# Graph layer with segment max: the dsts' clamp, the masks and the sum of x rearranged in the kernel's front

## The chip, the cores and the metric

The kernel runs on one core of a Trainium2 chip. Its engines work side by side, each through its own list of instructions in order: TensorE (PE in the profile, with its weight loads as PEld), VectorE (DVE), ScalarE (ACT), GpSimd (POOL) and SyncE (SP), which here only starts transfers. An engine waits where an instruction needs a semaphore that another engine or a transfer sets. The metric is the device time of one execution in microseconds. The kernel before took 811.47 us as the median of 3 runs (811.27 to 813.49).

## The reference

The input x has 6250 nodes of 128 channels. There are 206,250 edges as two lists, src and dst, sorted by dst (both directions of 100,000 random edges, and one self edge for each node). With W of 128 x 256 and b of 128:

```python
h = jnp.maximum(_layernorm(x, axis=-1), 0.0)
x_i, x_j = h[dst], h[src]
feat = jnp.concatenate([x_i, x_j - x_i], axis=-1)
msg = feat @ W.T + b
out = jax.ops.segment_max(msg, dst, num_segments=x.shape[0])
return x + jnp.where(jnp.isfinite(out), out, 0.0)
```

Split W into its halves W1 and W2. Then a message is A[dst] + B[src] + b with A = h (W1 - W2)^T and B = h W2^T. A[dst] + b is the same for all edges of a node, so the result is x + A + b + the maximum of B over the node's sources. The kernel computes A and B for all nodes once; the rest is a maximum over gathered rows.

## The kernel before, in words

**Tiling.** Node rows lie in a tile `xs` (the first 125 partitions of HX) as 125 partitions of Q = 50 nodes each, loaded in five groups of ten columns (`GQ`). For the edges, each of the 128 partitions owns LD = 49 consecutive nodes and reads a window of WIN = 1792 consecutive edges, which holds all its edges. Edges whose src is no duplicate within a look-back of POS = 44 go into one-hot matrices, which the main loop turns into B columns by matmuls; duplicates, at most 512 in a window, go into lists and are handled by gathers of B rows.

**Order.** The schedule is manual: each engine's instructions stand in the order of the text. The front (up to 177 us) does, with names and lines of the profile:

- *Constants* on POOL and VectorE: identities `ident`, `identb`, the negated `nid` and `nidb` (scaled by 1024), iotas, and `crow` and `rows_` (L317 to L321), one-partition rows for the selection table `Sel`.
- *Windows.* The last dst of each of 375 blocks is read (L330 to L341), a block is gathered, the count of smaller dsts gives the window's beginning (L386 to L391), and two gathers fetch `swin` (srcs) and `dwin` (dsts). `after` (L266) writes one element of the next x columns from the data that has just come, so that the x load behind it waits for that data: the second group of ten columns behind the block, groups three to five behind `dwin`.
- *Moments.* `moments` (L352) computes mean and variance of ten columns on VectorE, `roots` the square root on ScalarE, `scales` the reciprocal. Groups one and two run before the first comparison, three to five between comparisons.
- *Layernorm steps.* `ln_to(n)` issues steps up to number n. Step k works on five pairs of columns at once, as a pipeline: `ln_rest` of pair k-4, `ln_mul` of k-3, `ln_low` of k-2, `ln_turn` of k-1, `ln_scale` of k. `ln_mul` multiplies a split into a high and a low part by a split W, ten matmuls of 256 columns (L477), adds x through an identity matmul (L478), and ScalarE copies the results to `Bp`, the store buffer `b2` and, as A + b + x, back into `xs`. After each fifth pair SP stores ten columns of B to Bt and of `xs` to XA. 29 steps in all.
- *Keys and comparisons.* ScalarE forms `dlf` = dst - 49 p + 1 in place (L516); VectorE clamps it to 0..50 as `dlc` (L519), splits src into quotient and rest (`q16`) and packs dst and rest into a 16-bit key `KA`, with a copy `KB` shifted by one place. For each of 44 distances VectorE compares the keys with themselves (L552) into one of three buffers, and `count` adds the result into `dup` in PSUM by four matmuls (L541). Two masks are counted with weight -1024 so that marked places never pass as duplicates: `out_` (edges of other partitions' nodes) and `selfm` (self edges, L561), both after the 44 comparisons.
- *Lists.* `res` = (dup > 0) (L571), a running count, and eleven shift steps (L592, L593) pack the duplicates to the left; a one-column matmul with `tri` gives each partition's offset, which VectorE reads at the ninth step (L596). The lists are scattered to memory (`Lt`, L607, from POOL) and read back as balanced rows (L612, L629), from which the 432 gathers of the main loop take their indices. `turned` transposes q16, dlc and the values into TQ, TD, TV for the one-hots (`build`, L148).
- *Checks.* `same`, `junk` and others (L650 to L697) count violations of what the kernel assumes of the data; a sum above zero starts a slow general path.

**The main loop** (325 pairs) makes one-hots, multiplies them with Bp, takes maxima in `acc` on VectorE and streams 432 gathered duplicate rows. XA is read at the end and added.

Of the kernel before, what the change touches and what calls it, by code (L numbers as in the profile page):

```python
# [8 lines left out]
F32 = mybir.dt.float32  # L9
F32R = mybir.dt.float32r  # L10
BF16 = mybir.dt.bfloat16
# [4 lines left out]
ALU = mybir.AluOpType  # L16
# [34 lines left out]
def gnn_kernel(tc, x, src, dst, W, b, out):  # L51
# [28 lines left out]
    with ExitStack() as ctx:  # L80
# [20 lines left out]
        with ExitStack() as body:  # L101
# [137 lines left out]
            with ExitStack() as pre:  # L239
# [64 lines left out]
                for i, v in enumerate((-0.5 * LD - 0.5, -0.25 * (LD * LD - 1), float(-L))):  # L304
                    G_.memset(shifts[:, i:i + 1], v)
# [10 lines left out]

                V.tensor_tensor(crow[:, 0], crow[:, 0], crow[:, 0], ALU.mult)  # L317
                V.tensor_scalar(crow[:, 0], crow[:, 0], -1.0, 1.0, op0=ALU.mult, op1=ALU.add)
                V.tensor_scalar(crow[:, 1], crow[:, 0], -2047.0, -2048.0, op0=ALU.is_lt, op1=ALU.mult)
                V.tensor_tensor(rows_[:, 3], crow[:, 0], crow[:, 1], ALU.subtract)  # L320
                V.tensor_copy(rows_[:, 2], crow[:, 1])  # L321
# [46 lines left out]
                brow = pool.tile([P, 2 * C], F32R, name="brow")  # L368
# [14 lines left out]
                V.tensor_tensor(brow[32:33, C:], bsrc[32:33], brow[32:33, C:].bitcast(F32), ALU.subtract)  # L383
# [3 lines left out]
                after(V, blk_f[:1], GQ)  # L387
# [10 lines left out]


# [34 lines left out]

# [5 lines left out]
                V.memset(lw[96:], 0.0)  # L440
# [29 lines left out]
                def ln_mul(k):  # L470
                    st = steps[k]
                    st["pm"] = ps_m.tile([P, 2, 2 * C], F32, name="pm")
                    for j in range(2):
                        o = st["pm"][:L, j]
                        hi, lo = (slot(i, k)[:, j, :L] for i in (1, 2))
                        for a, w in ((bsel, brow), (hi, whi), (hi, wlo), (lo, whi), (lo, wlo)):
                            T_.matmul(o, a, w, start=j == 0 and a is bsel, stop=True, skip_group_check=True)  # L477
                    T_.matmul(st["pm"][:L, :, C:], ident[:L, :L], xs[:, 2 * k:2 * k + 2], start=False, stop=True,  # L478
                              skip_group_check=True)
# [28 lines left out]
                dlf = dwin.bitcast(F32)  # L508
# [7 lines left out]
                A_.activation(dlf, dwin, AF.Identity, bias=nthr)  # L516
                V.tensor_scalar(v16, big, MAGIC, -MAGIC, op0=ALU.add, op1=ALU.add)
                V.scalar_tensor_tensor(q16, v16, float(-Q), swin, op0=ALU.mult, op1=ALU.add)
                V.tensor_scalar(dlc, dlf, 0.0, float(LD + 1), op0=ALU.max, op1=ALU.min)  # L519
# [23 lines left out]
                for s in range(1, POS + 1):  # L543
                    e = eqs[s % 3]
                    if s in (12, 24):
                        turned(*((q16, TQ) if s == 12 else (dlc, TD)))
# [6 lines left out]
                    count(identb, e, first=s == 1)  # L553
                    for g, s0 in ((2, 8), (3, 14), (4, 20)):
# [5 lines left out]
                    ln_to(6 + 9 * s // POS)  # L560
# [378 lines left out]
```

## Time and profile before

| | us |
|---|---|
| median of 3 runs | 811.47 |
| the profiled execution | 809.35 |
| its span, first to last instruction | 807.6 |
| VectorE busy | 734.2 (91%) |
| TensorE busy | 662.4 (82%) |
| ScalarE busy | 511.8 (63%) |
| GpSimd busy | 502.5 (62%) |
| start of the first comparison (L552) | 37.39 |
| start of `res` (L571) | 101.63 |
| start of the scatter of the lists (L607) | 149.09 |
| end of the checks on VectorE | 177.0 |

Times in the profile count from the first instruction. A row of a timeline gives start, duration in us, engine, line, operation, output and input, and in brackets the idle time before it on its engine with what ended that. In the chain of waits a row is start, duration and what ran; it follows one chain back from the last instruction. Matmuls overlap one another, so their durations add up to more than the time between their starts.

### The profile page before, as it was taken

How to read it: one execution, taken by the hardware profiler on the slowest of the kernel's cores; microseconds unless marked ns; L12 is line 12 of the kernel's file. 1: busy time of each engine (PE TensorE's matmuls, PEld its weight loads, DVE VectorE, ACT ScalarE, POOL GpSimd, SP SyncE). 2: the span in 40 equal slices, each digit the busy share in tenths (PEclk: the TensorE clock that was granted, in tenths of full speed). 3: DMA queues.
4: the chain of work that ended last, by engine and by line, in shares of the span. 5: the costliest groups of instructions: out<-in, count | busy, mean ns of one | idle time of the engine just before them, and what ended most of it. 6: DMA issues, size and time to landing. Idle time of an engine off the chain costs nothing.

```text
span 807.6 us, 12060 instructions
## 1 busy us (share of the span) xinstructions
PE 662.4 (82%) x3646; PEld 434.2 (54%) x3646; DVE 734.2 (91%) x1368; ACT 511.8 (63%) x1130; POOL 502.5 (62%) x538
## 2 busy tenths in 40 slices
PE   1688977259898998799989998989989999989950
PEld 0455766138765565455555555555555555556730
DVE  6698899888789899999999999999999999998972
ACT  2664487046789999667575766666576666657800
POOL 5200000377777777777777777777777777774773
PEclk9999999559999899799999999999999999999975
DMA  4631222312333333333333373333343333334152
GB/s 126 178 106 46 64 65 71 99 47 79 93 87 105 102 105 101 106 104 102 102 102 105 101 190 106 101 103 103 107 114 105 108 105 103 102 104 124 54 161 84
DMA packets 79650, 82.09 MB, mean 102 GB/s; under 512 B 11699, under 2 KB 68503, under 8 KB 79223
## 3 DMA queue, kind: packets, MB, share of 16 engines
q1 hardware_dynamic: 63038, 46.54, 20.4%
q0 software_dynamic: 15840, 33.93, 14.8%
q10 hardware_dynamic: 700, 0.78, 0.5%
q8 instruction: 30, 0.49, 0.2%
q14 instruction: 42, 0.34, 0.1%
HBM read 42.34 MB, written 38.82 MB: 100 GB/s over the span
## 4 chain that ended last, share of the span: by engine, by line
DVE 41%; PE 23%; issue 17%; ACT 10%; DMA 5%; POOL 2%; DVEq 0%; POOLq 0%; SPq 0%; ACTq 0%
DVE acc L798 16%; PE ps L787 10%; DVE rows L223 9%; ACT oh L739 4%; PE z L738 4%; PE dup L541 3%; DVE acc L593 3%; DMA rows<-Bt,lists 3%; PE pv L189 2%; DMA rows<-M,last_e 2%; ACT dump L810 2%; POOL rows L77 1%; ACT Vb L199 1%; ACT Vsq L198 1%; DVE acc L592 1%
## 5 line engine op out<-in xcount | busy, mean ns | idle before, releaser
L77 POOL DMA_INDIRECT rows<-Bt,lists x432 | 437.2, 1012 | 137.4 <-DMA rows<-Bt,lists 44.5
L739 ACT ACTIVATE oh<-z 126x490 fp32r<-126x490 f32 (+1 forms) x650 | 336.7, 574 | 156.7 <-PE z L738 149.6
L787 PE MATMUL ps<-oh,Bp 126*128 126x490 f32 (+1 forms) x1300 | 390.2, 423 | 23.4 <-DVE acc L798 16.2
L798 DVE TENSOR_TENSOR acc<-acc,ps 128x980 f32<-128x980 f32 (+1 forms) x312 | 359.2, 1151 | 23.4 <-PE ps L787 19.7
L787 PEld LDWEIGHTS ps<-oh,Bp 126*128 126x128 f32 x1300 | 235.3, 193 | 147.5 <-DVE acc L798 90.7
L738 PE MATMUL z<-Vb,Sel 128*128 128x490 f16 (+1 forms) x650 | 194.7, 378 | 14.7 <-ACT oh L739 8.8
L223 DVE SCALAR_TENSOR_TENSOR rows<-rows,lists 128x128 f32<-128x128 f32 x431 | 148.0, 343 | 1.4 <-DMA rows<-Bt,lists 0.4
L189 PEld LDWEIGHTS <-HX 128*128 128x128 bf16 x896 | 68.3, 159 | 52.7 <-issue 37.3
L189 PE MATMUL pv<-HX 128*128 128x28 bf16 (+1 forms) x826 | 74.0, 232 | 16.2 <-ACT Vb L199 16.2
L607 POOL DMA_INDIRECT Lt<-big,where_i x1 | 1.0, 1037 | 120.4 <-DVE big L606 120.4
L738 PEld LDWEIGHTS <-Sel 128*128 128x128 f16 x650 | 43.1, 104 | 55.5 <-issue 53.9
L166 DVE TENSOR_TENSOR HX<-T,IQ 128x700 bf16<-128x700 bf16 x128 | 65.5, 515 | 0.0
L77 POOL DMA_INDIRECT rows<-M,last_e x40 | 38.2, 956 | 12.2 <-issue 7.0
L541 PE MATMUL dup<-rows,identb 128*128 128x512 bf16 (+1 forms) x176 | 36.7, 352 | 4.4 <-DVE rows L552 3.9
L810 ACT ACTIVATE dump<-lists,nbias 128x512 bf16<-128x512 f32 x50 | 37.0, 741 | 0.1
L541 PEld LDWEIGHTS <-identb 128*128 128x128 bf16 x176 | 17.0, 97 | 21.2 <-issue 6.1
L552 DVE TENSOR_TENSOR rows<-KA,KB 128x1792 bf16<-128x1792 int16 x22 | 23.8, 1082 | 3.7 <-PE dup L541 3.7
L477 PE MATMUL pm<-whi,lhl 128*125 128x256 f32 x100 | 26.6, 287 | 0.0
L477 PE MATMUL pm<-wlo,lhl 128*125 128x256 f32 x100 | 26.5, 287 | 0.0
L552 DVE TENSOR_TENSOR rows<-KA 128x1792 bf16<-128x1792 int16 x21 | 22.8, 1085 | 1.4 <-PE dup L541 1.4
L454 ACT ACTIVATE rows<-HX,nmr,rstd 125x128 f32<-125x128 f32 x50 | 22.8, 525 | 1.1 <-DVE rows L440 1.1
L173 DVE TENSOR_TENSOR HX<-HX,T 128x392 bf16<-128x392 bf16 x64 | 23.2, 363 | 0.3
(239 smaller groups left out, 564.4 us busy)
## 6 DMA issues: line engine op xcount, KB each, us to landing
M<-rows SPq DMA_DIRECT2D x54, 512.0 KB
rows<-Bt,lists POOLq DMA_INDIRECT x432
HX<-in_x SPq DMA_DIRECT2D x5, 560.0 KB
Bt<-acc SPq DMA_DIRECT2D x5, 560.0 KB
XA<-HX SPq DMA_DIRECT2D x5, 560.0 KB
out_x<-rows SPq DMA_DIRECT2D x4, 448.0 KB
xa<-XA SPq DMA_DIRECT2D x1, 1512.0 KB
T<-XA SPq DMA_DIRECT2D x1, 1176.0 KB
```

The costliest lines, as they stand in the source:

```text
L77: G_.indirect_dma_start(out=o, out_offset=None, in_=table, in_offset=bass.IndirectOffsetOnAxis(ap=idx, axis=0))
L166: V.tensor_tensor(oh, over(TQ, z - a), iq, ALU.is_equal)
L189: T_.matmul(o2[:, :, lo:lo + w], OHQ[:, :, i], OHD[:, :, :, i], start=False, stop=True, skip_group_check=True)
L223: V.scalar_tensor_tensor(G[:, j], state["prev"], slim[:, k:k + 1], G[:, j], op0=ALU.min, op1=ALU.max)
L477: T_.matmul(o, a, w, start=j == 0 and a is bsel, stop=True, skip_group_check=True)
L541: T_.matmul(dup[:, c0:c1], m, e[:, c0:c1], start=first, stop=last)
L552: V.tensor_tensor(e, KA[:, 64:], i1, ALU.is_equal)
L738: T_.matmul(z[:, :n], Sel[:, Q - 1 - i - j], Vb[t % 2][:, :n], start=True, stop=True)
L739: A_.activation(oh[:, :n], z[:L + 1, :n], AF.Relu)
L787: T_.matmul(ps[:, j, :n], Bp[:, e, i + j], oh[j][:, :n], start=e == 0, stop=e == 1)
L798: V.tensor_tensor(a, a, ps[:, :, :n], ALU.max)
L810: A_.activation(dump, sdl, AF.Sign, scale=2.0, bias=nbias[:, c:c + 1], accum_out=ends[:, c:c + 1])
```

## The change

What it does, part by part:

- The second group of x's columns is loaded behind `dwin` like groups three to five, and its moments stand behind the first comparison; groups three, four and five behind comparisons 9, 17 and 25.
- The `crow` operations and the clearing of `lw` stand behind the window gathers on VectorE.
- `dlc` comes from the integer `dwin` by two VectorE operations and now reaches from 0.5 to 49.5; the key is 128 dlc + q16. ScalarE's pass in place is gone.
- ScalarE writes `sl16`, src - 49 p + 1 in 16 bits. `selfm` is a 16-bit comparison of dlc with it, at comparison 9; `out_` is counted at comparison 6. Both use the space of TV, so KB stays the key.
- XA is filled with x by two copies in memory, on SP ahead of the stores of Bt. The identity matmul goes, the bias row is twice as wide and one matmul serves both columns; `xs` becomes A + b, and POOL adds it to XA by transfers that accumulate.
- Four layernorm steps stand ahead of the first comparison and six among the comparisons, against six and nine; the rest follows behind them. The transposes of q16 and dlc follow the last step.
- The `same` operations stand behind the read-back of the lists. Two one-column operations on dlc go.

```diff
-                V.tensor_tensor(crow[:, 0], crow[:, 0], crow[:, 0], ALU.mult)
...
-                    A_.copy(brow[r:r + 1, C:], bsrc[r:r + 1])
+                    A_.copy(brow[r:r + 1], bsrc[r:r + 1].rearrange("r (o c) -> r o c", o=1).to_broadcast([1, 2, C]))
...
-                after(V, blk_f[:1], GQ)
...
+                V.tensor_tensor(crow[:, 0], crow[:, 0], crow[:, 0], ALU.mult)
...
+                V.memset(lw[96:], 0.0)
...
-                moments(GQ, 2 * GQ)
-                roots(GQ, 2 * GQ)
-                scales(GQ, 2 * GQ)
-                for q0 in range(2 * GQ, Q, GQ):
+                for q0 in range(GQ, Q, GQ):
                     after(G_, dwin, q0)
...
                 nc.sync.dma_start(M_v[:, 0], none)
+                for l0, l1 in ((0, N // P * P), (N // P * P, N)):
+                    o, i = (a[l0:l1].rearrange("(p r) c -> p (r c)", p=min(P, l1 - l0)) for a in (XA, x))
+                    nc.sync.dma_start(o, i)
...
+                    T_.matmul(st["pm"][:L, :, C:], bsel, brow, start=True, stop=True, skip_group_check=True)
                     for j in range(2):
-                        o = st["pm"][:L, j]
                         hi, lo = (slot(i, k)[:, j, :L] for i in (1, 2))
-                        for a, w in ((bsel, brow), (hi, whi), (hi, wlo), (lo, whi), (lo, wlo)):
-                            T_.matmul(o, a, w, start=j == 0 and a is bsel, stop=True, skip_group_check=True)
-                    T_.matmul(st["pm"][:L, :, C:], ident[:L, :L], xs[:, 2 * k:2 * k + 2], start=False, stop=True,
-                              skip_group_check=True)
+                        for a, w in ((hi, whi), (hi, wlo), (lo, whi), (lo, wlo)):
+                            T_.matmul(st["pm"][:L, j], a, w, start=False, stop=True, skip_group_check=True)
...
                             nc.sync.dma_start(Bt_l[p0:p1, q0:q0 + GQ], bo[p0:p1])
-                            nc.sync.dma_start(XA_l[p0:p1, q0:q0 + GQ], xs[p0:p1, q0:q0 + GQ])
+                            G_.dma_start(XA_l[p0:p1, q0:q0 + GQ], xs[p0:p1, q0:q0 + GQ], accum_op=ALU.add)
...
-                selfm = KB[:, :WIN].bitcast(BF16)
...
-                out_ = TV.rearrange("p s b -> p (s b)")
-                ln_to(4)
+                out_ = selfm = TV.rearrange("p s b -> p (s b)")
...
-                A_.activation(dlf, dwin, AF.Identity, bias=nthr)
...
-                V.tensor_scalar(dlc, dlf, 0.0, float(LD + 1), op0=ALU.max, op1=ALU.min)
-                V.scalar_tensor_tensor(KA[:, 64:], dlc, 64.0, q16, op0=ALU.mult, op1=ALU.add)
+                V.tensor_scalar(dlc, dwin, nthr, 0.5, op0=ALU.add, op1=ALU.max)
+                V.tensor_scalar_min(dlc, dlc, LD + 0.5)
+                V.scalar_tensor_tensor(KA[:, 64:], dlc, 128.0, q16, op0=ALU.mult, op1=ALU.add)
                 V.tensor_copy(KB[:, 64:], KA[:, 63:63 + WIN])
-                ln_to(6)
+                ln_to(4)
...
+                sl16 = sh_.bitcast(BF16)[:, :WIN]
+                A_.activation(sl16, swin, AF.Identity, bias=nthr)
...
-                    if s in (12, 24):
-                        turned(*((q16, TQ) if s == 12 else (dlc, TD)))
...
-                    count(identb, e, first=s == 1)
-                    for g, s0 in ((2, 8), (3, 14), (4, 20)):
+                    count(identb, e, first=s == 1, last=s == POS)
+                    if s == 6:
+                        count(nidb, out_)
+                    if s == 9:
+                        V.tensor_tensor(selfm, dlc, sl16, ALU.is_equal)
+                        count(nidb, selfm)
+                    for g, s0 in ((1, 1), (2, 9), (3, 17), (4, 25)):
...
-                    ln_to(6 + 9 * s // POS)
-                V.scalar_tensor_tensor(selfm, dlf, nthr, swin, op0=ALU.subtract, op1=ALU.is_equal)
-                count(nidb, out_)
-                count(nidb, selfm, last=True)
+                    ln_to(4 + 6 * s // POS)
...
                 ln_to(ln_steps)
+                turned(q16, TQ)
+                turned(dlc, TD)
...
+                same = junk = KB[:, :WIN].bitcast(BF16)
+                V.tensor_tensor(same[:, 1:], dlc[:, 1:], dlc[:, :WIN - 1], ALU.not_equal)
...
-                same, junk = KA[:, :WIN].bitcast(BF16), KB[:, :WIN].bitcast(BF16)
-                V.tensor_tensor(same[:, 1:], dlc[:, 1:], dlc[:, :WIN - 1], ALU.not_equal)
...
-                V.tensor_scalar(fl[:, 1:2], dlc[:, :1], 1.0, None, op0=ALU.is_lt)
-                V.tensor_tensor(fl[:, :1], fl[:, :1], fl[:, 1:2], ALU.add)
```

More of the change, by code (lines that the diff above doesn't have):

```diff
@@ L303, in gnn_kernel @@
                 G_.memset(rows_[:, 1], -1.0)
-                for i, v in enumerate((-0.5 * LD - 0.5, -0.25 * (LD * LD - 1), float(-L))):
+                for i, v in enumerate((-0.5 * LD - 0.5, 12.0 - 0.25 * LD * LD, float(-L))):
                     G_.memset(shifts[:, i:i + 1], v)
@@ L315, in gnn_kernel @@
                 V.tensor_copy(identb, ident)
-                V.tensor_tensor(crow[:, 0], crow[:, 0], crow[:, 0], ALU.mult)
[L318 to L321, printed above, removed]
                 nidb = pool.tile([P, P], BF16, name="nidb")
@@ L612, in gnn_kernel @@
                     nc.sync.dma_start(a, at(Lt, o, [[PT, P], [1, NS]]))
+                same = junk = KB[:, :WIN].bitcast(BF16)
+                V.tensor_tensor(same[:, 1:], dlc[:, 1:], dlc[:, :WIN - 1], ALU.not_equal)
+                V.tensor_tensor(same[:, 1:], same[:, 1:], selfm[:, :WIN - 1], ALU.mult)
+                V.tensor_scalar(same[:, :1], dlc[:, WIN - 1:], float(LD), None, op0=ALU.is_le)
+                V.tensor_tensor(same[:, :1], same[:, :1], selfm[:, WIN - 1:], ALU.mult)
+                A_.activation(same, same, AF.Copy, accum_out=badc[:, 8:9])
                 val = q16
@@ L646, in gnn_kernel @@
                     f()
-                same, junk = KA[:, :WIN].bitcast(BF16), KB[:, :WIN].bitcast(BF16)
-                V.tensor_tensor(same[:, 1:], dlc[:, 1:], dlc[:, :WIN - 1], ALU.not_equal)
-                V.tensor_tensor(same[:, 1:], same[:, 1:], selfm[:, :WIN - 1], ALU.mult)
-                V.tensor_scalar(same[:, :1], dlc[:, WIN - 1:], float(LD), None, op0=ALU.is_le)
-                V.tensor_tensor(same[:, :1], same[:, :1], selfm[:, WIN - 1:], ALU.mult)
-                A_.activation(same, same, AF.Copy, accum_out=badc[:, 8:9])
-                V.scalar_tensor_tensor(junk[:, 1:], dlf[:, 1:], 1.0, dlf[:, :WIN - 1], op0=ALU.mult, op1=ALU.is_lt,
+                V.scalar_tensor_tensor(junk[:, 1:], dwin[:, 1:], 1.0, dwin[:, :WIN - 1], op0=ALU.mult, op1=ALU.is_lt,
                                        accum_out=badc[:, 0:1])
```

11 lines of the change are left out of this document (7 added, 4 removed).

## The prediction

> **What bounds the kernel now.** I read the page's slices first, then the table by stage, then VectorE's instructions in order of time, then the chain that ended last. The stage table (columns: stretch, length, then busy time of each engine with its instruction count, granted clock, DMA share, GB/s) cuts the span where the change bites:
>
> ```profile
> 0.00:37.40 37.40, 12.88 (x56) 9.37 (x57) 24.77 (x84) 15.52 (x38) 15.29 (x52) 1.00 0.55 158
> 37.40:101.60 64.20, 57.58 (x358) 37.94 (x358) 57.44 (x113) 35.33 (x88) 0.00 (x0) 1.00 0.25 72
> 101.60:148.30 46.70, 30.05 (x206) 26.06 (x205) 45.64 (x39) 30.31 (x98) 0.00 (x0) 0.94 0.28 83
> 148.30:177.00 28.70, 10.42 (x100) 7.41 (x101) 25.15 (x87) 7.38 (x14) 18.96 (x19) 0.50 0.17 53
> 177.00:807.60 630.60, 551.45 (x2928) 353.47 (x2927) 581.24 (x1049) 423.22 (x895) 468.29 (x468) 0.95 0.38 105
> ```
>
> The last row is the main loop. The change touches nothing in it, so I let it keep its 630.6 us and ask only when it starts. Up to 177 us VectorE (the third engine column) is the busiest, but not alone: from 37.4 to 101.6 TensorE is as full (57.58 against 57.44). VectorE's timeline shows its idle places (in brackets: idle before, and who ended it):
>
> ```profile
> 33.54 1.09 DVE L519 TENSOR_SCALAR dlc<-dwin 128x1792 bf16<-128x1792 f32 x1 [5.81 <-ACT dwin L516]
> 37.39 1.09 DVE L552 TENSOR_TENSOR rows<-KA,KB 128x1792 bf16<-128x1792 int16 x1
> 77.90 1.09 DVE L552 TENSOR_TENSOR rows<-KA,KB 128x1792 bf16<-128x1792 int16 x1 [1.49 <-PE dup L541]
> 101.63 2.02 DVE L571 TENSOR_SCALAR KA<-dup 128x1792 bf16<-128x1792 f32 x1 [0.86 <-PE dup L541]
> 141.88 0.21 DVE L596 TENSOR_SCALAR S<-dup 128x1 f32<-128x1 f32 x1
> 147.55 0.75 DVE L606 SCALAR_TENSOR_TENSOR big<-lists,nres,big 128x512 f32<-128x512 f32 x1
> 154.96 0.61 DVE L629 TENSOR_TENSOR big<-big,KA 128x432 f32<-128x432 f32 x1 [2.34 <-DMA KA<-Lt]
> ```
>
> So the front waits 5.81 us for ScalarE's conversion of the dsts, later a few us for TensorE's counts, and 2.34 us for the lists' way through memory. The chain of the counting stage shows TensorE setting the pace, one layernorm step for five comparisons:
>
> ```profile
> 83.06 3.86 PE dup L541 x20
> 86.92 0.12 PE pm L492
> 87.04 1.21 PE pm L477 x10
> 88.25 0.43 PE pm L478 x2
> 88.68 0.12 PE pt L466
> 88.80 0.22 PE pt L460 x2
> 89.02 3.86 PE dup L541 x20
> ```
>
> After the comparisons the leftover steps run every 3.01 us, in a loop between two engines: TensorE starts a step when ScalarE has copied `xs` (L483), ScalarE starts when the last matmul (L478) is there:
>
> ```profile
> 110.37 0.38 PE L492 MATMUL pm<-Bp,nid 125*125 125x256 f32 x1 [0.68 <-ACT HX L483]
> 111.66 0.28 PE L477 MATMUL pm<-wlo,lhl 128*125 128x256 f32 x1
> 111.78 0.60 PE L478 MATMUL pm<-HX,ident 125*125 125x256 f32 x2
> 112.41 0.37 ACT L481 CAST Bp<-pm 125x256 fp32r<-125x256 f32 x1 [0.51 <-PE pm L478]
> 112.94 0.39 ACT L483 COPY HX<-pm 125x256 f32<-125x256 f32 x1
> ```
>
> **1. Up to the first comparison (37.39 us before).** Three things go: x's second ten columns are no longer loaded ahead of the two window gathers, their moments (19.30 to 22.8) leave, and VectorE clamps the integer dsts itself, without L516. The five `crow` operations move behind the gathers; L319 alone took 3.75 us while POOL's two iotas ran (3.26 to 6.92), and the matmul that L339 needs was done at 7.45, so about 0.4 is won there, less 0.14 for the wider bias operation. Between 16 and 22 us the DMAs moved 301 to 333 GB/s; 640 KB less ahead is 2.0 us, so the dsts land at 24.86 - 2.3 = 22.6, and the 917 KB of srcs 2.9 earlier, 19.7. VectorE is free for them by 17.4, or by 20.7 if POOL's iotas hold the moved `crow` operations as they held L319. I take 20.5; ends 19.7 and 23.0 (L515 started at 23.45 with the srcs already there). Then L515, L517, L518 take 4.3 by their starts. The new clamp is two operations: one like L519, 1.1 (integer input costs nothing extra: L515 reads integers in 1.09), and a bf16 minimum between L521's 0.63 and 1.09; I take 0.65 since L521 is also 16 bits in and out. L520 and L521 are 2.7. First comparison at 29.3, 8.1 earlier. ScalarE loses L516 and gains a 1.7 us conversion, all behind the comparisons.
>
> **2. The comparisons.** VectorE: 44 at 1.005 (start to start), 44.2; four groups of moments instead of three, each 2.94 (2.62 and 0.32 in the gaps at 45.41 and 50.01), 11.8; the 16-bit self mask 1.0 in place of 2.08 after the loop; x's second group may land late. Its load now waits for the dsts and for POOL's two small copies, each of which can sit behind one VectorE operation (L270 took 2.00 beside L518), then 4 to 5 us (the load issued at 14.3 was used at 19.30): ready at 30 to 34 against a need at 30.3. I take 0.8 for it (0 to 4) and 0.4 for the square root behind ScalarE's five window passes. Sum 58.3, so 87.6, and with `pk` (2.02) the count is read at 89.7. TensorE needs 44 x 0.772 + six steps of 1.65 + the two masks' 1.5 = 45.4 in that time, so it no longer sets the pace. In a step 0.12 (one bias matmul) and 0.43 (L478) are gone from 2.10. The two masks and both transposes leave the end of the loop. 89.7 against 101.63: 11.9 gained, 8.1 of it from part 1.
>
> **3. The leftover steps.** Fifteen steps are left instead of ten, then four draining ones, then the transposes of q16 and dlc. In the loop above L481 can start 0.56 earlier (last L477 0.12 earlier, ending 0.28 after its start, at 111.82 + 0.03 in place of 112.41), so a step takes 2.45; ScalarE's own work is 2.36 by its start-to-start times. Step 10 starts at 90.0, step 24 ends at 125.9, and only then comes the one-column matmul that L596 reads. VectorE wants it 40.25 after L571 (141.88 - 101.63), at 129.95: 4 us of cover. The transposes then end near 139; the build first needs them at 145. On ScalarE the sum of `same` (1.7) now stands ahead of the turned values' copies, which so end near 143, still in time.
>
> **4. The sum of x by DMA.** The identity matmul's work goes to ten accumulating DMAs on POOL, and two copies of x into XA (3.2 MB) on SP ahead of the Bt stores. At 300 GB/s and twice the traffic the copies are some 21 us, issued near 55: done before the second group's sum, and no consumer of Bt comes before 145. On POOL nothing is queued between the dsts' copies and the scatter L607, so waits there cost nothing until the last group. Its `xs` is there at 90.0 + 17 x 2.45 + 2.4 = 134.05. Two issues at 1.04 + 0.30 (L607's own time and a gather's gap) end at 136.8; VectorE ends L606 at 148.30 - 11.9 = 136.4, and POOL started 0.79 after that before, 137.2. So the issue fits by 0.4. The trace has no accumulating DMA: its price lies between nothing and gathers' slowest issue (2.02 twice, scatter 1.55 late) with 640 KB at 150 GB/s ahead of the scatter's data (4.3, about 2 of them late). I take 0.7, nearer the plain rows. VectorE's clearing of HX (L627, 142 us) waits for the same sums to have read `xs`; they would have landed by 140.
>
> **5. After the lists.** The `same` operations (166.25 to 168.76, 2.51 us) move into the wait for the lists. VectorE then has 2.5 + 4.4 of work there, so L629's addition starts at 136.4 + 6.66 + 0.7 = 143.8 and the 2.34 idle is filled. Lead 11.2. Later the 2.51 are missing, and two one-column operations, 0.3. The main loop starts 14.0 earlier.
>
> **Sum.** The profiled execution took 809.35 (span 807.6, 1.75 around it); minus 14.0 is 795.4. It lay 2.1 under the median of the runs, 811.47, from which I forecast 797.5.
>
> **The rivals.**
> (a) *The leftover steps become the bound.* If the loop keeps 3.01 because the wait on L483 or the copies set it, L596 waits until 134.2, the last `xs` comes at 144.1, the scatter at 146.8, and L629 at 152.7. Lead 2.3 + 2.8: 806.4. For it: 15 steps are left. Against: ScalarE idles 0.51 in every step for L478 alone.
> (b) *POOL's issues are held up by VectorE.* Gathers took 0.94 us at 171.9 but 1.82 and 2.02 at 167.46 and 169.58, beside L650, L651 and L656. With both last issues at 2.3 and the sum's data at half rate before the scatter's, the scatter lands 4 to 5 late: 802. The Trainium skill, "SBUF — State Buffer", section "Summary: rules for kernel authors", says to issue such a DMA from ACT or SP, since the software descriptors of GpSimd are starved while VectorE is in a fast mode; by that rule this rival holds, and the gathers' times here agree in direction.
> (c) *Slower: the accumulates back up.* Queue 0 runs them one after another, 12.25 us apart by the steps, and the scatter and all gathers stand behind them. If 640 KB takes more than 13.2 us (under 48 GB/s), starting at 85, the fifth ends past 151.2 and the whole lead is gone; at 14 us it ends at 155: 815. Against: XA's stores before shared 294 GB/s between 126 and 130 us. For: nothing here shows a read and write of the same bytes.
>
> **How the numbers follow.** The forecast 0.58, (a) 0.08, (b) 0.18, (c) 0.10, no measurable change 0.03 (several smaller losses meeting), better than 793 0.03. A gain of 2.4 us, 0.3%, is about what a measurement can tell. Forecast, (a), (b) and the better case are faster: 0.87. The likeliest case alone spans 794 (no late load, no late scatter, srcs at 19.7, 2.7 together) to 801 (srcs at 23.0 and the slow minimum, 3). With (a) and (b): 793 to 806.5.
>
> **What would show it.** First comparison near 29.3; hardly a VectorE wait on TensorE until the count is read near 89.7; steps every 2.45 us; the read of L596 not waiting; the scatter within 2 us of the lists' end; main loop at about 163 and 630 us long. Wrong if the dsts land no earlier, x's second group holds the moments, POOL is still issuing sums when the lists are ready, or the main loop itself changes length.

## The result and the profile after

The changed kernel takes 803.4 us (median of 6 runs, 801.8 to 806.67), the kernel before in the same session 811.73 (6 runs, 810.77 to 813.49). The ratio is 0.990, with a 95% interval of 0.9875 to 0.9926. The forecast was 797.5 with a range of 793 to 806.5: faster, as said, but by 8.3 us and not by 14.0. The profiled execution of the changed kernel took 805.83 (span 804.1), 2.4 above its median; that of the kernel before lay 2.4 below its own. So the two profiles differ by 3.5 us where the medians differ by 8.3, and stages are better compared than spans. In one session every kernel, the one before included, took about 1140 us at a granted clock near 0.8; of the three runs made there only the front is read.

| | before | after | predicted |
|---|---|---|---|
| first comparison | 37.39 | 30.18 | 29.3 |
| `res`, the count read | 101.63 | 90.80 | 89.7 |
| lists ready (end of L606, now L604) | 148.30 | 137.67 | 136.4 |
| addition to the lists (L629, now L634) | 154.96 | 148.34 | 143.8 |
| main loop starts | 176.95 | 167.45 | 163.0 |
| main loop, to the end of the span | 630.65 | 636.65 | 630.6 |

The same cut by stage, of the kernel after (stretch, length, busy time of PE, PEld, DVE, ACT and POOL with their instruction counts, granted clock, DMA share, GB/s):

```profile
0.00:30.18 30.18, 7.12 (x21) 4.45 (x22) 19.07 (x61) 12.94 (x26) 16.92 (x51) 1.00 0.39 117
30.18:90.80 60.62, 49.51 (x253) 27.25 (x258) 58.92 (x136) 20.36 (x49) 3.33 (x6) 1.00 0.52 146
90.80:137.67 46.87, 33.49 (x252) 29.10 (x251) 45.84 (x40) 44.38 (x144) 7.11 (x8) 1.00 0.42 89
137.67:167.45 29.78, 11.83 (x114) 8.46 (x114) 24.76 (x84) 10.35 (x19) 18.90 (x19) 0.52 0.35 83
167.45:804.10 636.65, 553.83 (x2928) 354.18 (x2927) 581.51 (x1049) 422.77 (x895) 469.78 (x470) 0.95 0.39 104
```

In the second row VectorE is busy for 58.92 of 60.62 us and TensorE for 49.51: VectorE alone sets the pace now. VectorE's timeline at the places that were shown of before:

```profile
21.42 1.09 DVE L509 TENSOR_SCALAR big<-rows 128x1792 f32<-128x1792 int32 x1 [3.33 <-DMA rows<-in_src,begin_i]
25.61 1.15 DVE L512 TENSOR_SCALAR dlc<-dwin,nthr 128x1792 bf16<-128x1792 int32 x1
30.18 1.09 DVE L546 TENSOR_TENSOR rows<-KA,KB 128x1792 bf16<-128x1792 int16 x1
32.09 2.03 DVE L348 BATCH_NORM_STATS2 stats<-HX 125x6 f32<-125x128 f32 x10 [0.82 <-DMA HX<-in_x]
77.46 1.09 DVE L546 TENSOR_TENSOR rows<-KA 128x1792 bf16<-128x1792 int16 x1 [0.30 <-PE dup L537]
90.80 2.01 DVE L567 TENSOR_SCALAR KA<-dup 128x1792 bf16<-128x1792 f32 x1
131.24 0.13 DVE L594 TENSOR_SCALAR S<-dup 128x1 f32<-128x1 f32 x1
136.92 0.75 DVE L604 SCALAR_TENSOR_TENSOR big<-lists,nres,big 128x512 f32<-128x512 f32 x1
148.34 0.61 DVE L634 TENSOR_TENSOR big<-big,KA 128x432 f32<-128x432 f32 x1 [3.95 <-DMA KA<-Lt]
```

The 5.81 us for ScalarE's conversion are gone, the waits for TensorE's counts are down to 0.3, and the read at L594 does not wait. But the wait at the end, for the lists' way through memory, has grown from 2.34 to 3.95, although 2.5 us of other work were moved into it. The leftover steps, TensorE's start and ScalarE's copies:

```profile
119.19 0.38 PE L489 MATMUL pm<-Bp,nid 125*125 125x256 f32 x1 [0.68 <-ACT HX L480]
121.65 0.38 PE L489 MATMUL pm<-Bp,nid 125*125 125x256 f32 x1 [0.68 <-ACT HX L480]
124.11 0.38 PE L489 MATMUL pm<-Bp,nid 125*125 125x256 f32 x1 [0.68 <-ACT HX L480]
```

```profile
120.67 0.37 ACT L478 CAST Bp<-pm 125x256 fp32r<-125x256 f32 x1
123.14 0.37 ACT L478 CAST Bp<-pm 125x256 fp32r<-125x256 f32 x1
```

A step takes 2.46 us against 3.01. ScalarE no longer idles before L478; TensorE waits for ScalarE, and ScalarE is full. Now the lists. POOL issues the last sums of x and then the scatter, SP the read-back:

```profile
124.57 2.44 POOL L485 DMA_DIRECT2D XA<-HX  x2 [10.66 <-ACT lhl L467]
136.86 1.67 POOL L485 DMA_DIRECT2D XA<-HX  x2 [9.85 <-issue]
138.84 1.93 POOL L605 DMA_INDIRECT Lt<-big,where_i  x1 [0.30 <-DVE KB L614]
```

```profile
145.26 0.34 SPq L610 DMA_DIRECT2D big<-Lt  x1
145.64 0.43 SPq L610 DMA_DIRECT2D KA<-Lt  x1
```

From the scatter's start to the first read-back 6.42 us pass; before it was 2.88 (149.09 to 151.97). What the DMA engines did meanwhile, in 40 slices of 0.4 us from 136 to 152 (the busy share in tenths, and what was moved):

```profile
DMA  0098987994489899998200000459940000000000
GB/s 0 0 320 243 307 282 307 269 77 51 90 179 205 179 192 218 208 264 320 105 21 20 0 0 0 56 117 367 393 173 0 0 0 0 0 0 0 0 0 0
```

The first full stretch (136.8 to 139.2) is the plain store of B, near 300 GB/s. The second (140.4 to 144) is the accumulating sum with the scatter in it: the engines are as busy, yet until 142.8 only some 180 to 220 GB/s pass. The read-back is issued after the last of that.

### The profile page after: what moved, and what is told of

It reads as the page before. It is cut to its first block, busy times and chain, and to the rows that moved or that the text cites. A ratio compares the mean times of both kernels' runs of the same rounds, so it can differ in the third digit from the quotient of the medians.

```text
span 804.1 us, 11914 instructions
## 1 busy us (share of the span) xinstructions
PE 655.8 (82%) x3566; PEld 423.4 (53%) x3571; DVE 730.1 (91%) x1366; ACT 510.8 (64%) x1130; POOL 516.0 (64%) x550
## 3 DMA queue, kind: packets, MB, share of 16 engines
q0 software_dynamic: 16640, 37.13, 19.1%
## 4 chain that ended last, share of the span: by engine, by line
DVE 39%; PE 21%; issue 17%; ACT 10%; DMA 9%; POOL 2%; DVEq 0%; POOLq 0%; SPq 0%; ACTq 0%
DVE acc L794 15%; PE ps L783 10%; DVE rows L223 8%; DMA rows<-Bt,lists 5%; PE z L734 5%; ACT oh L735 5%; DVE acc L591 3%; PE pv L189 2%; DVE rows L546 2%; ACT dump L806 2%; DMA rows<-M,last_e 2%; ACT Vb L199 1%; ACT Vsq L198 1%; PE dup L537 1%; DVE acc L590 1%
## 5 line engine op out<-in xcount | busy, mean ns | idle before, releaser
L734 PE MATMUL z<-Vb,Sel 128*128 128x490 f16 (+1 forms) x650 | 197.2, 381 | 14.5 <-ACT oh L735 8.5
L485 POOL DMA_DIRECT2D XA<-HX x10 | 9.9, 1215 | 96.9 <-issue 71.2
L537 PE MATMUL dup<-rows,identb 128*128 128x512 bf16 (+1 forms) x171 | 40.4, 370 | 17.5 <-DVE rows L546 16.1
L491 ACT CAST Bp<-pm 125x256 fp32r<-125x256 f32 x25 | 9.7, 388 | 35.6 <-PE pm L489 35.6
```

The lines of the kernel that those rows point to most:

```text
L537: T_.matmul(dup[:, c0:c1], m, e[:, c0:c1], start=first, stop=last)
L734: T_.matmul(z[:, :n], Sel[:, Q - 1 - i - j], Vb[t % 2][:, :n], start=True, stop=True)
```

## The experiments

Times of runs are given with their ratio to the kernel before in the same session. "Lists' way" means the time from the lists being ready to the start of the addition: 6.66 us in the kernel before, 10.67 in the changed one. The main loop's start is read from one profiled execution each.

**The clamp alone, in the kernel before.** VectorE clamps the integers, and ScalarE's pass moves behind the sixth step.

```diff
-                A_.activation(dlf, dwin, AF.Identity, bias=nthr)
...
-                V.tensor_scalar(dlc, dlf, 0.0, float(LD + 1), op0=ALU.max, op1=ALU.min)
+                V.tensor_scalar(dlc, dwin, nthr, 0.0, op0=ALU.add, op1=ALU.max)
+                V.tensor_scalar_min(dlc, dlc, float(LD + 1))
...
                 ln_to(6)
+                A_.activation(dlf, dwin, AF.Identity, bias=nthr)
```

> The kernel before with one part of the change alone: VectorE clamps the integer dsts by two operations, and ScalarE's pass over the dsts stands behind layernorm step 6. Theory: the 5.81 us of idle time ahead of the clamp go, so the first comparison starts near 32.3 in place of 37.39, but then TensorE, with nine steps of 2.10 among the comparisons, sets the pace: the count is read only 2 to 3 us earlier than at 101.63, the run takes about 809. Rival: the 5 us pass through to the end, 806.6.

Measured: 810.1 us, ratio 0.9979 (0.9965 to 0.9993). The first comparison starts at 32.38, 5.0 earlier, but the count is read only 1.6 earlier. The counting stage of this kernel by stretch, and VectorE's longest and last wait in it:

```profile
32.38:100.05 67.67, 59.88 (x372) 40.49 (x378) 57.53 (x113) 40.08 (x99) 0.01 (x1) 1.00 0.31 89
```

```profile
49.06 0.22 DVE L363 RECIPROCAL rstd<-rstd 125x10 f32<-125x10 f32 x1 [2.49 <-ACT rstd L359]
100.05 2.02 DVE L572 TENSOR_SCALAR KA<-dup 128x1792 bf16<-128x1792 f32 x1 [0.86 <-PE dup L542]
```

TensorE has the larger sum (59.88 against 57.53), with nine steps and the transposes still among the comparisons, and VectorE's waits for it add up to 7.5 us (6.7 in the kernel before). But its longest wait, 2.49 us, is for ScalarE's square root: ScalarE does five passes over the windows and a layernorm step first, one of the passes being the one that the edit put there, so the square root starts at 48.70 (48.14 in the kernel before) although VectorE is earlier. So both engines take from the lead, and how much TensorE alone would have taken was not separated. In the kernel before, the clamp by itself is worth 1.6 of its 5 us.

**ScalarE converts, VectorE clamps in one operation (in the changed kernel).**

```diff
-                V.tensor_scalar(dlc, dwin, nthr, 0.5, op0=ALU.add, op1=ALU.max)
-                V.tensor_scalar_min(dlc, dlc, LD + 0.5)
+                A_.activation(big, dwin, AF.Identity, bias=nthr)
+                V.tensor_scalar(dlc, big, 0.5, LD + 0.5, op0=ALU.max, op1=ALU.min)
```

> The changed kernel with the dsts converted by ScalarE again (into a free tile, as the next thing behind the first four layernorm steps), and clamped by one VectorE operation. Theory: the gain at the front came from where the conversion stood, behind four steps that ended at 31.7; in the changed kernel those steps end near 25.4, so ScalarE converts from 25.4 to 27.2, the clamp ends near 28.3 in place of 27.43 and the first comparison comes at 31.0 to 31.3 in place of 30.18: a loss of 1. Rival: ScalarE's pass was the cost itself; the first comparison comes 4 to 5 later, near 35.

Measured: 810.5 us, ratio 0.9980 (0.9965 to 0.9996), first comparison at 30.74, main loop from 174.24. The edit did not make the kernel that the expectation describes: it put the conversion ahead of the four layernorm steps in ScalarE's order, not behind them. ScalarE's and VectorE's lines:

```profile
25.06 1.79 ACT L512 ACTIVATE big<-dwin,nthr 128x1792 f32<-128x1792 int32 x1 [8.86 <-DMA dwin<-in_dst,begin_i]
26.75 0.86 ACT L453 ACTIVATE rows<-HX,nmr,rstd 125x128 f32<-125x128 f32 x2
42.44 0.29 ACT L353 ACTIVATE rstd<-mv,eps 125x10 f32<-125x10 f32 x1
```

```profile
42.76 0.21 DVE L357 RECIPROCAL rstd<-rstd 125x10 f32<-125x10 f32 x1 [6.01 <-ACT rstd L353]
```

VectorE hardly waits for the conversion itself (0.59 us). The first comparison is 0.56 late, as the srcs were (22.01 against 21.42); from the srcs on it takes 8.73 us, against 8.76 in the changed kernel. The cost comes behind it: ScalarE idles 8.86 us for the dsts, does its four steps afterwards and then the five passes over the windows, and the square root for the second group's moments comes last, so VectorE stands still for 6.01 us in the middle of the comparisons. What the pass cost was its place in ScalarE's order.

**x's second group loaded ahead of the gathers again.**

```diff
                 V.tensor_copy(blk_f, blk)
+                after(V, blk_f[:1], GQ)
...
-                for q0 in range(GQ, Q, GQ):
+                for q0 in range(2 * GQ, Q, GQ):
```

> The changed kernel with x's second group loaded behind the block again, ahead of the two window gathers, as in the kernel before. The prediction's step: 640 KB ahead cost the gathers 2.0 us, so the srcs' pass moves from 21.42 to 23.4 and the first comparison from 30.18 to 32. Theory now: the dsts landed at 24.94 in the changed kernel and 24.86 in the one before, so the gathers don't share in that cost; the first comparison stays within 1 us of 30.2, the moments' wait of 0.82 for x goes, the time stays within 1.5 us of 803.

Measured: 803.28 us, ratio 0.9887 (0.9869 to 0.9906), the same as the changed kernel. The srcs are read at 22.66 instead of 21.42 (their gather was issued 0.67 later, too), the dsts are there at 25.06 instead of 24.94, and the wait of 0.82 us for x is gone. The first comparison starts at 31.43, 1.25 later than in the changed kernel, which is more than the 1 us that was expected: 0.67 is the later issue and 0.57 the srcs' longer way. By the time the count is read (91.48 against 90.80) only the 0.68 of the issue is left. So the moved load gains some 0.6 us on the srcs and gives it back among the comparisons. The DMA engines from 12 to 28 us (0.4 us a slice) show why, first the kernel before, then the one after:

```profile
DMA  3000000084799899889989869895300000000000
GB/s 132 0 0 0 0 0 0 0 128 102 256 422 333 243 251 241 233 323 448 394 340 323 305 287 412 358 379 215 161 36 18 0 0 0 0 0 0 0 0 0
```

```profile
DMA  0000000000000446999969399898410000000008
GB/s 0 0 0 0 0 0 0 0 0 0 20 0 0 90 90 233 376 394 448 394 161 233 108 233 358 358 448 376 179 72 36 0 0 0 0 0 0 0 0 90
```

In both kernels the two gathers are issued at 15.9 and 17.2. Before, the DMA engines were moving x from 15.2 on; after, next to nothing moves until 17.2. In the kernel before some 500 of the 640 KB went through by 17.2, while the gathers' own data had not begun to flow. Without x's data there is also a gap near 20 to 21 us (108 to 233 GB/s), and the last bytes come at the same time as before.

**The sum undone: the identity matmul and SP's stores again.**

```diff
-                    nc.sync.dma_start(o, i)
+                    pass
...
+                    T_.matmul(st["pm"][:L, :, C:], ident[:L, :L], xs[:, 2 * k:2 * k + 2], start=False, stop=True,
+                              skip_group_check=True)
...
-                            G_.dma_start(XA_l[p0:p1, q0:q0 + GQ], xs[p0:p1, q0:q0 + GQ], accum_op=ALU.add)
+                            nc.sync.dma_start(XA_l[p0:p1, q0:q0 + GQ], xs[p0:p1, q0:q0 + GQ])
```

> The changed kernel with the sum of x by DMA undone: the identity matmul is back, SP stores XA, x is not copied to XA first. Theory: the 15 leftover steps run every 3.01 again, step 24 ends near 135, VectorE waits about 4 us for the offsets (read at 131.24 in the changed kernel), the last stores stand on SP ahead of the read-back of the lists, and the addition of the lists starts near 151.5 in place of 148.34: about 806.5. Rival: the sums are a pure cost on the scatter's queue; without them the lists come 3.5 us earlier and the run takes about 800.

Measured: 808.24 us, ratio 0.9961 (0.9946 to 0.9975), main loop from 172.05. The steps take 2.90, and VectorE waits for them and then for the lists:

```profile
135.73 0.16 DVE L596 TENSOR_SCALAR S<-dup 128x1 f32<-128x1 f32 x1 [4.25 <-PE dup L577]
146.15 2.02 DVE L623 SCALAR_TENSOR_TENSOR q<-dup,lists 128x1792 bf16<-128x1792 f32 x1 [1.61 <-PE ptb L533]
152.93 0.61 DVE L636 TENSOR_TENSOR big<-big,KA 128x432 f32<-128x432 f32 x1 [2.70 <-DMA KA<-Lt]
```

So the sum by DMA is worth 4.8 us (808.24 less 803.4), by keeping TensorE's and ScalarE's loop short enough for 15 leftover steps. The read-back is late here too (issued at 148.72, behind SP's last stores), though nothing accumulates.

**Plain writes in place of the sums.** `accum_op=ALU.add` is left out of the ten transfers, so this kernel's output lacks x.

> The changed kernel with the ten transfers of the sum as plain writes from GpSimd, not accumulating (the output lacks x, as the rows of XA are overwritten with A + b). Theory: an accumulating transfer moves its bytes at about half the rate (some 160 to 200 against 300 GB/s), so a plain one leaves the queue some 2 us sooner and the addition of the lists starts near 146.3 in place of 148.34. Rival: it is the place in the queue alone, the addition stays at 148.

Measured: 800.29 us (one run). POOL's lines:

```profile
138.33 1.04 POOL L485 DMA_DIRECT2D XA<-HX  x2 [10.75 <-issue]
139.77 1.23 POOL L605 DMA_INDIRECT Lt<-big,where_i  x1 [0.40 <-issue]
```

The pair of issues takes 1.04 us instead of 1.67, the data pass at 300 GB/s, and the lists' way is 8.51: scatter to read-back 4.70 where the sums made it 6.42 and nothing in the way 2.88. The addition itself starts only at 147.56, not near 146.3 as expected, since the lists were ready 1.4 later than in the changed kernel. By this one profile, of the 4.0 us lost about half belongs to 640 KB of data standing there at all, half to its being accumulated.

**The last group's sums behind the scatter, and behind the first forty gathers.** Two kernels. In both the last group is left out of the loop; its two transfers are issued right after the scatter in the one, after the first forty gathers in the other.

```diff
-                            G_.dma_start(XA_l[p0:p1, q0:q0 + GQ], xs[p0:p1, q0:q0 + GQ], accum_op=ALU.add)
+                            if q0 + GQ < Q:
+                                G_.dma_start(XA_l[p0:p1, q0:q0 + GQ], xs[p0:p1, q0:q0 + GQ], accum_op=ALU.add)
...
+                for p0, p1 in PARTS:
+                    G_.dma_start(XA_l[p0:p1, Q - GQ:], xs[p0:p1, Q - GQ:], accum_op=ALU.add)
```

> The changed kernel with the last group's two accumulating transfers issued on GpSimd behind the scatter of the lists, not ahead of it. Theory (the scatter's data stand behind the sum's data in the same queue): the read-back is issued about 2.9 us after the scatter's start again, as in the kernel before, the addition of the lists starts near 144.6 in place of 148.34, and the run is 3.5 us faster, near 800. Rival (the scatter is slow from VectorE's hold on the descriptors or from the stores of Bt): the addition stays at 147 or later and the time at 803.

> The changed kernel with the last group's two accumulating transfers issued behind the first forty gathers of the main loop, past both the scatter and the read-back. Theory (whatever of the lists' way comes beside the last sum's data waits for it; behind the scatter it held the read-back): the addition starts as soon as VectorE is free, near 144.6, the main loop 3.5 us earlier, time near 800. Rival: the lists' way is slow for another reason and the addition stays at 147 or later, 803.

Measured: 802.85 us, ratio 0.9889 (0.9872 to 0.9906), and 802.13, ratio 0.9872 (0.9851 to 0.9892). VectorE's addition in the first of the two, then in the second:

```profile
148.64 0.61 DVE L637 TENSOR_TENSOR big<-big,KA 128x432 f32<-128x432 f32 x1 [3.37 <-DMA KA<-Lt]
```

```profile
145.53 0.61 DVE L635 TENSOR_TENSOR big<-big,KA 128x432 f32<-128x432 f32 x1 [0.59 <-DMA KA<-Lt]
```

Behind the scatter the scatter is quick (3.14 us to the read-back), but then the sums' data meet the read-back, a load from SP on another queue: 6.17 us instead of 3.0. The expectation missed this. The wait only moved, and the lists' way is still 10.13. Behind the gathers it is 6.97, and the main loop starts at 164.64, 2.8 earlier than in the changed kernel. The median is only 1.3 lower; with four runs from 801.28 to 804.47 it is open whether the main loop gave the rest back.

**Nine steps among the comparisons instead of six, spread evenly.** If the last sums are issued earlier, they are through before the scatter.

```diff
-                    ln_to(4 + 6 * s // POS)
+                    ln_to(4 + 9 * s // POS)
```

> The changed kernel with nine layernorm steps among the comparisons in place of six. Theory (TensorE has 58 - 45 us to spare there): the count is still read near 90.8, the leftover loop ends 7.4 us earlier, the last sum is through before the scatter, the addition of the lists starts near 144.5 and the run takes about 800. Rival: TensorE sets the pace among the comparisons again, VectorE waits, the count is read 2 us or more later, and the run takes 802 to 805.

Measured: 801.65 us, ratio 0.9872 (0.9842 to 0.9902). The sums are out of the way (issued at 133.34, scatter at 141.56, lists' way 6.82), but VectorE waits 4.1 us for TensorE and reads the count at 94.47. The main loop starts at 167.19, only 0.3 earlier than in the changed kernel, so the front does not explain a median that is 1.75 lower; the intervals of the two ratios overlap. The two longest of VectorE's waits on the result buffers:

```profile
43.60 1.09 DVE L546 TENSOR_TENSOR rows<-KA,KB 128x1792 bf16<-128x1792 int16 x1 [1.05 <-PE dup L537]
54.11 1.09 DVE L546 TENSOR_TENSOR rows<-KA 128x1792 bf16<-128x1792 int16 x1 [1.49 <-PE dup L537]
```

Between 30 and 91 us TensorE idles 16.0 us waiting for comparisons in this kernel (16.1 in the changed one), so it has time, but not where these steps stand. Part of the 4.1 us may be the clock's: from 51 to 54 us, just ahead of the longest wait, the granted clock was 0.50 in this profile and 1.00 in that of the changed kernel. With three buffers it can neither get ahead of VectorE nor fall more than a few comparisons behind.

**The three extra steps at the moments.** VectorE gives TensorE nothing during the 2.9 us of each group's moments; the steps stand there.

```diff
-                    ln_to(4 + 6 * s // POS)
+                    ln_to(4 + 6 * s // POS + (s >= 9) + (s >= 17) + (s >= 25))
```

> The changed kernel with three more layernorm steps among the comparisons, one each at comparisons 9, 17 and 25, where VectorE does the moments and feeds TensorE nothing. The theory (TensorE's spare time lies in those 2.9 us alone, so steps that stand there cost VectorE nothing, and the last sums are issued three steps, 7.4 us, earlier): VectorE's waits for TensorE's counts stay at 1 or less, the duplicates are read at 91 to 91.5, the last xs is there near 129, both last sums are through before the scatter, scatter to read-back's issue about 3, the addition to the lists at 144.5 to 145.5, main loop from 163.5 to 165, time 799 to 801. The rival (three buffers let the count of a distance reach no further back than the comparison three earlier, so any step costs VectorE its length wherever it stands): duplicates read at 93 or later, the addition at 147 or later, time 802 to 803.

> The changed kernel with the same three steps at the moments and, beside that, the last group's two accumulating transfers behind the first forty gathers. If the three steps alone already take the sums out of the lists' way, this one gives nothing more: the addition to the lists and the main loop's start within 0.5 of the kernel with the steps alone, 799 to 801. If the sums still meet the scatter or the read-back there, it starts the main loop 1 to 3 earlier than that kernel.

> The changed kernel once more, as the yardstick for the two beside it. First comparison near 30.2, duplicates read near 90.8, scatter to read-back's issue about 6.4, main loop from about 167.4; time 802 to 804, main loop about 634 long by the medians.

These three came to 1146.23, 1133.38 and 1144.04 us beside 1136.56 (1113 to 1154) for the kernel before, so their times say nothing of the edits. The lists' way and the main loop's start are 6.81 and 164.25 with the steps placed, 6.80 and 163.23 with the sums behind the gathers as well, and 10.83 and 168.43 in the changed kernel. The last sums and the scatter on POOL with the steps placed:

```profile
129.88 1.67 POOL L485 DMA_DIRECT2D XA<-HX  x2 [10.04 <-issue]
138.27 1.68 POOL L605 DMA_INDIRECT Lt<-big,where_i  x1 [6.72 <-DVE big L604]
```

As the theory has it, but for VectorE's waits for TensorE, which are 1.4 us and not 1 or less: the count is read at 91.20, and the sums are done before the scatter; then moving them behind the gathers adds nothing to the lists' way. The 1.0 by which that kernel's main loop starts earlier was there before the lists were ready (137.32 against 137.97) for the most part. The steps placed were run once more:

> The kernel with three more layernorm steps at the moments, a second time, since the three runs before it came to 1133 to 1146 us, as the kernel before itself did beside them, and say nothing of its time. Where the kernel before takes its 811 again: the theory (the front is 4.2 shorter, as in its first profile, and the main loop has its 633 to 635 by the medians) gives a main loop from 163.7 to 164.5 and 799 to 801; the rival (what the front gains the main loop gives back, as with the last group's sums behind the gathers) 802 to 803.

Measured: 798.61 us (5 runs, 797.93 to 801.11) against 812.0, ratio 0.9835 (0.982 to 0.985). That is better than the changed kernel (0.9875 to 0.9926), and the fastest that was run with all of the work in it. In its profile the count is read at 91.98 (the srcs came 1.2 later than in this kernel's first profile), the main loop starts at 164.58, and the end of the front is:

```profile
139.00 1.68 POOL L605 DMA_INDIRECT Lt<-big,where_i  x1 [6.67 <-DVE big L604]
```

```profile
145.45 0.61 DVE L634 TENSOR_TENSOR big<-big,KA 128x432 f32<-128x432 f32 x1 [0.37 <-DMA KA<-Lt]
```

The lists' way is 6.75 us, what it was in the kernel before, with the 2.5 us of `same` work inside it. VectorE waits 1.3 us for TensorE here, although the granted clock was 0.50 for a while (36 to 40 us). Of the 4.8 us by which the median is below the changed kernel's, 2.9 are in the front of the profiles; the rest is in the main loop and unexplained.

## Why the prediction was right, and where it was off

Faster was right, by 1.0% where 1.7% was forecast, and the median lies within the range; the likeliest case was too good by 5.9 us. The shorter clamp, the relief of TensorE and the shorter steps worked as described. Two of the signs that the prediction named for being wrong did appear: the dsts landed no earlier (24.94 against 24.86), and POOL was still issuing sums when the lists were ready (until 138.53, against 137.67). In size the result is nearer to rival (b), 802, than to the forecast, and it lies in the range because the range made room for (a) and (b). By the table, the main loop starts 4.5 later than forecast. That is 0.9 up to the first comparison, 0.2 in the comparisons, 0.2 up to the lists and 3.3 on the lists' way; behind that the front is as long as forecast (19.1 us). The rest of the 5.9 is the main loop, and 0.3 by which the kernel before was slower in these runs than in those first shown.

**1, up to the first comparison.** The term that failed is the 2.0 us for x's 640 KB. The dsts landed at 24.9 and not at 22.6. The step took the bytes ahead of the gathers as time ahead of them; the DMA rows and the run with x early show that most of those bytes went through before the gathers' data began to flow. The srcs came at 21.42 (20.5 taken, ends 19.7 to 23.0), and from there the chain of VectorE was as priced: 8.76 us to the first comparison against 8.8 forecast (1.15 and 0.63 for the clamp against 1.1 and 0.65). Had the srcs come sooner, no more than 0.7 was to be had, since the dsts landed at 24.94 and the clamp of them began at 25.61.

**2, the comparisons.** 60.62 against 60.4, the wait for x's second group 0.82 against 0.8, VectorE's waits for TensorE 0.7 in all. The prediction's own terms (44.2, 11.8, 1.0, 0.8, 0.4 and 2.02) add up to 60.2, and 2.10 less 0.12 and 0.43 is a step of 1.55, not 1.65; the first slip moves the forecast by 0.2, the second by nothing. The clamp alone shows that it needed the other parts: without them 5.0 us of lead shrink to 1.6, by waits for TensorE and for ScalarE.

**3, the leftover steps.** 2.46 against 2.45, and L594 does not wait. Step 10 started at 92.13 and not at 90.0: 1.1 because the count was read later, and 1.0 because the sixth step among the comparisons is issued behind the last of them (89.67) and still ran. So the one-column matmul was issued at 128.19, and the cover was about 3 us and not 4. With the identity matmul back a step is 2.90 and the wait 4.25: rival (a)'s world, at 808.24 where (a) said 806.4.

**4, the sum by DMA.** The price of 0.7 was the mis-sized term: the lists' way grew by 4.0, more than the 1.55 and 2 of the upper bound together. Of this, 0.4 is the scatter's later start (1.17 after the lists are ready, against 0.79), 0.9 its longer issue (1.93 against 1.04), and 2.6 the longer time from there to the read-back, in which the sum's data pass; whether the longer issue would have cost anything without those data was not separated. The prediction compared instants of issue ("the issue fits by 0.4") and let most of the data pass unpriced, though its own upper bound had 4.3 us of data in it. It also put the last `xs` at 134.05; it was complete at 136.35, mostly for the two reasons under 3. This is rival (b) in its amount, with one of its two causes: the data went at about 0.6 of a plain store's rate, but the last two issues took 1.67 together, where (b) had both at 2.3.

The same pair of issues took 1.04 as plain writes and 1.67 as sums, beside the same VectorE work, so that difference is not VectorE's. The rule that the prediction named, from the Trainium skill, "SBUF — State Buffer", section "Summary: rules for kernel authors", is that GpSimd's software descriptors are starved by VectorE's fast modes. The scatter agrees with it in direction: with no sums ahead it took 1.04 beside a pass of 2.02 us (the kernel before) and 1.14 to 1.68 beside passes of 1.09 (the sums behind it, and the steps placed). But the slowest gather that the prediction cites for it, 2.02 us at 169.58, stood beside L656, which takes 2.02 us where L650 takes 1.08. The remedy of that rule, to issue from ACT or SP, is not open to a sum: by the Trainium skill, "DMA: Bandwidth & Descriptors", section "SWDGE vs HWDGE vs iDMA", accumulating transfers are GpSimd's alone, which no run here tests.

Rival (c) fell: the fourth group's 640 KB, issued at 124.57, were through by 132.

**5, after the lists.** The `same` work hid as said, but the wait it was to fill is 3.95 and not gone, for the reason under 4. With the sums out of the way the wait is 0.37 to 0.59, near the forecast of none.

**The main loop.** The prediction left it at 630.6. Taken by medians (median, less 1.75 around the span, less the start), it is 633.0 in the kernel before, 634.2 after, and 632.3 in the last run with the steps placed. The two profiles alone would say that 6.0 us were lost in it. The starts are of one profile each, so differences of 1 us between these lengths are not clear of noise. At the twelve places where a tile's first maximum is taken (L796, now L792) the lead is 10.0 to 11.3 for the first nine, then 8.5, 7.9 and 4.2. In two late stretches the clock that was granted differs, in the kernel before, then after:

```profile
598.00:645.00 47.00, 43.14 (x235) 26.82 (x236) 46.74 (x89) 30.92 (x63) 36.03 (x37) 1.00 0.37 105
690.00:740.00 50.00, 44.98 (x223) 27.87 (x221) 46.31 (x77) 34.03 (x71) 31.54 (x33) 1.00 0.43 118
```

```profile
598.00:645.00 47.00, 42.97 (x229) 26.50 (x228) 45.31 (x84) 30.06 (x60) 36.26 (x36) 0.96 0.37 97
690.00:740.00 50.00, 43.32 (x205) 26.49 (x204) 42.67 (x66) 30.17 (x62) 30.28 (x32) 0.97 0.41 110
```

The fastest run of the changed kernel has the highest mean clock and the slowest the lowest (801.8 at 0.949, 806.67 at 0.930), but 802.51 and 805.83 both stand at 0.943. Whether the change has any part in when the clock dips was not settled; no run held the front and varied the main loop alone.

## What to carry to other kernels

Price a transfer by when its bytes move, not by when it is issued: here bytes ahead of a load cost next to nothing while the load's own data had not begun, and bytes in the way of a short round trip that VectorE waited for cost about the time that they took to move, whether that was the scatter on POOL's queue or the read-back on SP's. Work moved to an engine with spare time must stand where that time is: with three more steps spread evenly VectorE waited 4.1 us, with the three at the moments 1.3 to 1.4, and 0.7 without them. An instruction in an in-order queue that waits for late data delays everything behind it, so look at the work behind a moved operation as well as at the operation.

## What the runs showed of the hardware that was not expected

- A transfer from SBUF that accumulates into memory kept the DMA engines as busy as a plain store and moved less: 172 GB/s at a busy share of 0.93 (128 to 130 us, the fourth group's sum), against 297 GB/s at the same share for the stores of the kernel before. The last pair of issues on POOL took 1.67 us where plain writes took 1.04; the pairs before it took 1.66 to 2.44.
- Such a sum under way held back a plain load that SP had issued: the lists' read-back took 6.17 us instead of 3.0. The Trainium skill, "DMA: Bandwidth & Descriptors", section "Issuing engines are not separate DMA queues", says that all transfers interleave on the same 16 engines whoever starts them, and this agrees; the expectation of that run had left it out.
- POOL's one-element and 29-element copies that release x's loads took 0.59 to 2.03 us each while VectorE worked on the keys, and 0.17 to 0.18 while it stood idle (31.3 to 32.1 us in the changed kernel, from 27.7 us in the one before).
